# Feed-forward weight rounding placed from 3.0 instead of from 0 in a planned transformer layer

## The chip, the cores and the metric

The kernel runs on one core of a Trainium2 chip. The time is the device time of one launch in microseconds (us), as the median of several runs; lower is better. The core has a matrix engine (TensorE, PE in the profile, with its weight loads as PEld), a vector engine (DVE), a scalar engine (ACT), a general engine (GpSimd, POOL) and SyncE (SP), which here issues nearly all transfers. Every engine takes its instructions in the order in which they were traced. TensorE's clock is throttled at times, and the profile gives the granted share as PEclk.

## The reference, cut to what matters

One pre-norm layer on x of shape (2, 2048, 256): causal attention with 16 heads of 16, and a gated feed-forward of width 704, whose weights and inputs are rounded to blockwise FP4 values.

```python
x = x + attn(layernorm(x), Wq, bq, Wk, bk, Wv, bv, Wo, bo)   # rope on q and k, causal softmax
x = x + ffn(layernorm(x), w_gate, w_up, w_down)

def fp4_quant_dequant(x):            # blocks of 16 along the last dimension
    scale = max(max(abs(block)) / 6, 1e-12)
    q = nearest of (0, .5, 1, 1.5, 2, 3, 4, 6) to abs(block / scale), with its sign
    return q * scale
def fp4_linear(x, w):
    return fp4_quant_dequant(x) @ fp4_quant_dequant(w).T
h = silu(fp4_linear(x, w_gate)) * fp4_linear(x, w_up)
return fp4_linear(h, w_down)
```

## The kernel before, in words

**Tiling.** The sequence of each of the two batches b is cut into four chunks c of 512 rows (CH), each chunk into four tiles of 128. The 16 heads are in four groups g of four heads. A (batch, chunk, group) is one slot of the attention; there are 32 slots. A slot has two passes over the keys. The maximum pass (`max_steps`) multiplies queries and keys (`sc`, L1068, masked by L1037) and reduces each product to a row maximum on DVE (`mx` in chunk 0, `parts` in the others, L1092); the maxima are split in two parts (`mslots`, L1130 and L1133), turned (`ptm`, L1149) and copied (`mT`, L1153). The value pass (`value_steps`) computes the scores again less the maxima (`sx`, L1200 and L1208), takes the exponential on ACT (`ex`, L1223) and multiplies by the values (`av`, L1256).

**What a slot needs first.** Chunk by chunk, and in two blocks of eight heads each (blk), queries and keys are projected (`project_steps`): the matmul `pj` (L812), the bias on ACT (`qb`, L825), the cosine part on DVE (`t`, L832), a shuffle on DVE (L858), the sine part, a sum and a remainder on POOL (L864, L867, L894), then a trip through DRAM on the SP queue (`parts`, L904, and from there `qT`, L915, and `kT`, L928). The values are copied on DVE (`v`, L1003). The input rows are normalised in `norm_steps`, on DVE and POOL (`rstd`, L524).

**Rounding of the weights.** The three feed-forward weights are cut into 18 pieces (`weight_items`): six of `w_gate`, six of `w_up` and six of `w_down`, mostly 128 x 256. `load_rounded` gives each piece four steps: load (SP, `wr`, L649), scaled (DVE: L558, L561, L562; POOL: L566, L569), rounded (DVE: L585, L588; POOL: L591, L594, L597) and turn (two transposes on PE, `ptr`, L660, and copies on ACT, L680 or L690). A piece holds one of two buffers of kind `xn` from its load to its turn; the feed-forward of the rows uses the same two buffers later. The first matmul that reads a rounded weight is `pg` (L1548), in the feed-forward of the first chunk.

**The planner.** Nothing is issued at once. Each step calls `add` with an engine, an estimated cost, what it reads and writes, and a due place on one common list. `Plan.ordered` then goes through all tasks: it lets each engine take a task that can begin first, by its own estimates of costs, transfer landings (`landing`, 2.0 us and 1 us for each 250 KB) and free buffers; among those that can begin within PATIENCE = 0.03 us of the first, the lowest due goes first. A task is a candidate only if its due is at most AHEAD = 3 above the lowest due not yet done. The order found is the order of tracing, so on the chip each engine keeps it, whether the estimates held or not.

**Places.** Places are numbers, not microseconds. Slot n's maximum pass covers the places from `place[n]` to `place[n+1]`, its value pass begins 0.3 of a slot after that. The costs in the code give place 0 to 0.4 for slot 0, 0.4 to 1.4, 1.4 to 2.4 and 2.4 to 3.4 for slots 1 to 3 (the first chunk), 3.4 to 4.8 for slot 4, 4.8 to 6.8 for slot 5 and 6.8 to 8.8 for slot 6. Projections are placed between the slots that need them, for instance the first chunk's second block at 0.12 to 0.9 and the second chunk's first block at 1.7 to 2.9. The opening work has places from -10 to about -7. The 18 pieces are spread over 0 to WEIGHTS = 8: piece i covers a width of 1.9 shares from i shares, and one share is 8/19 = 0.42. The first chunk's feed-forward starts at place 8.2.

The change is in `layer_kernel`, in the lines that place the pieces:

```python
items = weight_items()
share = WEIGHTS / (len(items) + 1)
for i, steps in enumerate(items):
    side += placed(steps, i * share, (i + 1.9) * share)
```

Of the kernel before, what the change touches and what calls it, by code (L numbers as in the profile page):

```python
# [83 lines left out]
LATE = 4  # L84

WEIGHTS = 8

NUDGE = 1.0 - 1.5 * 2.0**-23

# [217 lines left out]
def layer_kernel(  # L307
# [364 lines left out]
    def weight_items():  # L672

        items = []
        for w, wT, target in ((w_gate, wgT, wg_), (w_up, wuT, wu_)):
            for row in range(0, I, P):
                rows = min(P, I - row)

                def put(pt, wT=wT, row=row, rows=rows):
                    nc.scalar.copy(wT[:, :, row : row + rows], pt[:, :, :rows])  # L680

                items.append(load_rounded(w, row, rows, 0, E, put, target))
        for row in range(0, E, P):
            for col in range(0, I, E):
                cols = min(E, I - col)

                def put(pt, row=row, col=col, cols=cols):
                    for k in range(0, cols, P):
                        n = min(P, cols - k)
                        nc.scalar.copy(  # L690
                            wdT[:n, (col + k) // P, row : row + P], pt[:n, k // P, :]
                        )

                items.append(load_rounded(w_down, row, P, col, cols, put, wd_))
        return items
# [991 lines left out]
    def placed(steps, lo, hi):  # L1687

        lags = [lag for lag, _ in steps]
        lags[0] = 0  # L1690
        at, out = 0, []
        for lag, step in zip(lags, (step for _, step in steps)):
            at += lag
            out.append((lo + (hi - lo) * at / max(sum(lags), 1), step))
        return out
# [17 lines left out]
    for n in range(slots):  # L1713
        steps, split, turn = max_steps(*order[n // NG], n % NG)
# [4 lines left out]
        steps, divide = value_steps(*order[n // NG], n % NG)  # L1719
# [6 lines left out]
    side = []  # L1726
# [10 lines left out]
        side += placed(project_steps(*order[k], blk), lo, hi)  # L1737
        done = hi
    items = weight_items()
    share = WEIGHTS / (len(items) + 1)  # L1740
    for i, steps in enumerate(items):
        side += placed(steps, i * share, (i + 1.9) * share)
    raw_o = []
    side.append((0.2, lambda due: raw_o.extend(load_plain(wo, "y", att, due))))
    side.append(
# [8 lines left out]
    ready = [divided[NG * k + NG - 1] + 0.01 for k in range(len(order))]  # L1754
    ready[0] = max(ready[0], WEIGHTS + 0.2)
    end = place[slots + 1]
    at = 0
    for k in range(len(order) - 1):
# [8 lines left out]
        share = (at - lo) / TPC  # L1767
# [37 lines left out]
    steps = [step for _, step in project_steps(*order[0], 0)]  # L1805
# [11 lines left out]
    def transpose_biases(due):  # L1817
# [46 lines left out]
        lambda due, i=i, pair=pair: steps[0].stripped(i, pair, due)  # L1864
# [73 lines left out]
```

## Time and profile before

| what | value |
|---|---|
| median of three runs (lowest to highest) | 1386.13 us (1380.96 to 1386.45) |
| time of the profiled execution | 1382.78 us |
| its span in the profile | 1381.0 us |
| PE busy | 1311.1 us, 95% of the span |
| DVE busy | 1115.0 us, 81% |
| ACT busy | 749.6 us, 54% |
| POOL busy | 538.2 us, 39% |
| mean granted clock of TensorE | 0.969 |
| first scaling of a weight piece on DVE (L558) | 24.8 us |
| last transpose of a weight piece (L660) | 174.5 us |
| first `pg` matmul (L1548) | 195.8 us |

The profiled execution's time is its span and 1.78 us around it. Busy time is a mean over stages with different limits, so the stage in which the weights are rounded, the first 175 us, has to be read by itself. The windows view gives, for each stretch, the busy time of each engine with the number of instructions, then the granted clock, the share in which the transfer engines were busy, and what they moved.

### The profile page before, as it was taken

Reading aid. Unit: us, or ns where it says so; the run is one execution under the profiler, and the core shown is the slowest. Engines: PE = TensorE matmul, PEld = TensorE weight load, DVE = VectorE, ACT = ScalarE, POOL = GpSimd, SP = SyncE. Lnnn points to the kernel's source line nnn. Section 1 sums busy time; section 2 is a strip of 40 time slices with the busy share of each in tenths; the row PEclk is TensorE's granted clock in tenths of the full one; section 3 lists DMA queues with packets and bytes.
Section 4 is the critical chain, followed back from the end, with each engine's and each line's share of the span. In section 5 each row is a group of like instructions: output and inputs, shape, how many; then the busy total and the mean of one; then the engine's idle time right before and its main releaser. Section 6 shows DMA issues by size and latency. Waiting matters only on the chain.

```text
span 1381.0 us, 27458 instructions
## 1 busy us (share of the span) xinstructions
PE 1311.1 (95%) x10269; PEld 653.7 (47%) x10269; DVE 1115.0 (81%) x2415; ACT 749.6 (54%) x1670; POOL 538.2 (39%) x685
## 2 busy tenths in 40 slices
PE   7887999999999999999998999999999999999977
PEld 4443454444544444444454555444454444444455
DVE  7787989988889998875478888996878978884286
ACT  3532655456655566557743555454655556667711
POOL 4654635434323434314344644432342332321360
PEclk8977999999999999999999999999999999999998
DMA  2544433321121401221444414240130130000000
GB/s 88 133 124 109 100 89 63 100 40 55 56 47 39 109 17 39 66 51 44 93 112 96 108 38 99 70 93 24 47 85 18 42 81 13 5 14 9 9 1 19
DMA packets 61886, 84.37 MB, mean 61 GB/s; under 512 B 14772, under 2 KB 30520, under 8 KB 61752
## 3 DMA queue, kind: packets, MB, share of 16 engines
q1 hardware_dynamic: 61744, 82.61, 24.4%
q8 instruction: 81, 1.33, 0.4%
q14 instruction: 53, 0.43, 0.1%
q10 hardware_dynamic: 8, 0.00, 0.0%
HBM read 55.09 MB, written 27.49 MB: 60 GB/s over the span
## 4 chain that ended last, share of the span: by engine, by line
PE 65%; DVE 20%; issue 5%; POOL 5%; DMA 2%; ACT 2%; SPq 0%; POOLq 0%; DVEq 0%; ACTq 0%
PE av L1256 15%; PE sc L1068 9%; PE pg L1548 9%; PE sx L1200 8%; DVE parts L1092 8%; PE sx L1208 7%; PE pd L1642 6%; PE pj L812 3%; PE pth L1407 2%; PE po L1492 2%; PE pv L994 1%; DVE scale L558 1%; DVE step L585 1%; PE sc L1037 1%; DVE step L588 1%
## 5 line engine op out<-in xcount | busy, mean ns | idle before, releaser
L1223 ACT ACTIVATE ex<-sx 128x512 f32<-128x512 f32 (+3 forms) x1280 | 592.6, 539 | 346.8 <-PE sx L1208 203.0
L1092 DVE TENSOR_REDUCE parts<-sc 128x1 f32<-128x512 f32 (+3 forms) x1152 | 638.5, 613 | 65.2 <-PE sc L1068 46.3
L1208 PE MATMUL sx<-qT,kT 64*128 64x512 f32 (+3 forms) x1280 | 338.0, 524 | 0.0
L1256 PE MATMUL av<-ex,v 128*32 128x512 f32 (+3 forms) x2560 | 301.1, 543 | 0.0
L1068 PE MATMUL sc<-kT,qT 64*128 64x512 f32 (+3 forms) x1280 | 288.6, 431 | 12.9 <-DMA kT<-parts 3.4
L1200 PE MATMUL sx<-mT,less 64*128 64x512 bf16 (+3 forms) x1280 | 250.7, 357 | 5.9 <-DVE parts L1092 2.2
L1068 PEld LDWEIGHTS sc<-kT,qT 64*128 64x128 f32 x1280 | 137.7, 191 | 173.0 <-DVE parts L1092 57.0
L1200 PEld LDWEIGHTS <-less 64*128 64x128 bf16 x1280 | 67.8, 94 | 212.4 <-issue 203.2
L566 POOL TENSOR_SCALAR inv<-inv 128x16 f32<-128x16 f32 (+2 forms) x82 | 17.6, 215 | 369.4 <-DVE inv L562 341.2
L1208 PEld LDWEIGHTS sx<-qT,kT 64*128 64x128 f32 x1280 | 133.2, 197 | 10.3 <-issue 7.7
L1642 PE MATMUL pd<-wdT,hrT 128*128 128x256 f32 (+1 forms) x384 | 104.8, 414 | 1.3 <-ACT hrT L1411 0.8
L1256 PEld LDWEIGHTS av<-ex,v 128*32 128x32 f32 x2560 | 52.7, 108 | 70.9 <-issue 60.5
L1642 PEld LDWEIGHTS pd<-wdT,hrT 128*128 128x128 f32 (+1 forms) x384 | 70.5, 198 | 29.5 <-issue 15.8
L864 POOL TENSOR_TENSOR t<-t,cs 128x512 f32<-128x512 f32 x31 | 39.8, 1285 | 112.3 <-DVE t L858 106.3
L1548 PE MATMUL pg<-wgT,xT 128*128 128x352 f32 x224 | 76.9, 476 | 0.9 <-ACT xT L1411 0.8
L812 PE MATMUL pj<-xnT,wqkT 128*128 128x512 f32 x128 | 74.1, 674 | 3.6 <-DVE v L1003 1.7
L1092 DVE TENSOR_REDUCE mx<-sc 128x1 f32<-128x128 f32 (+3 forms) x128 | 54.5, 479 | 26.4 <-PE sc L1037 26.2
L1548 PE MATMUL pg<-wuT,xT 128*128 128x352 f32 x224 | 74.4, 472 | 0.1
L1037 PE MATMUL sc<-pick,mask_q 64*128 64x64 bf16 x1024 | 70.5, 201 | 0.0
L591 POOL TENSOR_TENSOR h<-h,step 128x704 f32<-128x704 f32 x28 | 47.2, 1687 | 48.8 <-DVE step L588 41.0
L1037 PE MATMUL sx<-pick,mask_k 64*128 64x64 bf16 x1024 | 64.4, 198 | 0.0
L1574 ACT ACTIVATE h<-pg 128x352 f32<-128x352 f32 x64 | 29.8, 466 | 62.9 <-PE pg L1548 54.8
(156 smaller groups left out, 1534.2 us busy)
## 6 DMA issues: line engine op xcount, KB each, us to landing
qT<-parts SPq DMA_DIRECT2D x120, 128.0 KB
kT<-parts SPq DMA_DIRECT2D x120, 128.0 KB
parts<-high SPq DMA_DIRECT2D x30, 256.0 KB
parts<-t SPq DMA_DIRECT2D x30, 256.0 KB
sums<-avs SPq DMA_DIRECT2D x28, 256.0 KB
cs<-in_rope_dram SPq DMA_DIRECT2D x8, 512.0 KB
xin<-in_L_attn_x_dram SPq DMA_DIRECT2D x28, 128.0 KB
y<-sums SPq DMA_DIRECT2D x28, 128.0 KB
```

The costliest lines, as they stand in the source:

```text
L591: queue.tensor_tensor(src(), src(), st["step"], ALU.add)
L812: nc.tensor.matmul(got["pj"], lhsT=wqkT[:, k, i, cols], rhs=xnTs[b, c][:, k, :], start=(k == 0), stop=(k == KE - 1),)
L864: (nc.gpsimd if early and i == 0 else queue).tensor_tensor(swapped, swapped, angles[b, c][:, 1, :], ALU.mult)
L1037: nc.tensor.matmul(sc[h][:, col + at : col + at + STRIP], lhsT=strips(mask, h, half), rhs=strips(pick, h), start=False, stop=(half == 1),)
L1068: nc.tensor.matmul(sc[h][:, :cols], lhsT=strips(qT, h, d, slice(i * P, (i + 1) * P)), rhs=strips(kT, h, duo, slice(0, cols)), start=True, ...
L1092: nc.vector.tensor_reduce(dst, got[0][h][:, :cols], AX.X, ALU.max)
L1200: nc.tensor.matmul(sc[h][:, off:], lhsT=strips(less[d], h), rhs=strips(mT, h, slice(off, CH)), start=True, stop=False,)
L1208: nc.tensor.matmul(sc[h][:, off:], lhsT=strips(kT, h, duo, slice(jj, jj + P)), rhs=strips(qT, h, d, slice(off, CH)), start=False, stop=(j ...
L1223: nc.scalar.activation(st[j, d][:, h, off:], got[0][h][:, off:], AF.Exp, scale=HD**-0.5)
L1256: nc.tensor.matmul(st["av"][SLOT * s : SLOT * (s + 1), off:], lhsT=v[:, at : at + SLOT], rhs=st[j, d][:, h, off:], start=(j == 0), stop=(j ...
L1548: nc.tensor.matmul(got[half], lhsT=split("xrT")[:, k, :], rhs=wT[:, k, half * IH : (half + 1) * IH], start=(k == 0), stop=(k == KE - 1),)
L1642: nc.tensor.matmul(st["pd"], lhsT=st["hrT"][:n, k, :], rhs=wdT[:n, k, :], start=(k == 0), stop=(k == KI - 1),)
```

## The change

A constant FIRST = 3.0 is added. The 18 pieces are now spread over 3 to 8 instead of 0 to 8: one share is 5/19 = 0.263 instead of 0.421, and a piece's own four steps cover 0.5 instead of 0.8. Piece 0 goes from the places 0 to 0.8 to the places 3.0 to 3.5, piece 8 from 3.37 to 4.17 to 5.11 to 5.61, and piece 17 from 7.16 to 7.96 to 7.47 to 7.97. Steps, instructions, tiles and buffers are the same; only the dues that the planner sees differ.

```diff
 WEIGHTS = 8
+
+FIRST = 3.0
...
     items = weight_items()
-    share = WEIGHTS / (len(items) + 1)
+    share = (WEIGHTS - FIRST) / (len(items) + 1)
     for i, steps in enumerate(items):
-        side += placed(steps, i * share, (i + 1.9) * share)
+        side += placed(steps, FIRST + i * share, FIRST + (i + 1.9) * share)
```

## The prediction

> **What bounds the kernel now.** I read the page first. Over the span TensorE is the bound: PE is busy for 1311.1 of 1381.0 us, and what is left is little.
>
> ```profile
> span 1381.0 us, 27458 instructions
> ...
> PE   7887999999999999999998999999999999999977
> ...
> DVE  7787989988889998875478888996878978884286
> ...
> POOL 4654635434323434314344644432342332321360
> PEclk8977999999999999999999999999999999999998
> ```
>
> One digit is 34.5 us. PE falls short in the first four digits and the last two, and the clock in the first four. The change works in the first five, so I cut that stretch with the windows view at the events that matter: the first maximum reductions (24 us), the first key products of slot 2 (72), of slot 4 (107), the end of slot 4's maximum pass (about 138), the last weight transpose (175).
>
> ```profile
> 24.00:72.00 48.00, 40.36 (x350) 22.08 (x347) 33.43 (x90) 22.72 (x56) 28.85 (x42) 0.84 0.45 107
> 72.00:107.00 35.00, 32.09 (x316) 17.99 (x316) 29.40 (x77) 16.40 (x43) 20.14 (x29) 0.76 0.52 121
> 107.00:118.70 11.70, 8.18 (x39) 4.11 (x40) 6.15 (x18) 1.41 (x4) 5.54 (x9) 0.71 0.64 152
> 118.70:138.00 19.30, 13.84 (x73) 7.52 (x70) 18.96 (x44) 3.20 (x8) 5.83 (x11) 0.65 0.28 78
> 138.00:175.00 37.00, 34.72 (x304) 16.20 (x303) 34.67 (x90) 24.57 (x62) 25.16 (x42) 1.00 0.45 97
> ```
>
> The columns after the length are PE, PEld, DVE, ACT, POOL, then clock, transfer share and GB/s. From 24 to 107 no engine is full: PE idles 10.6 us, DVE 20.2 us. From 118.7 to 138 DVE is full (18.96 of 19.30) and PE idles 5.5 us at a clock of 0.65: here only the maximum pass of slot 4 can run. From 138 to 175 PE and DVE are both full (2.3 us idle each).
>
> **What a piece costs.** In the groups view up to 200 us the 18 pieces cost DVE 7.0 (L558) + 7.0 (L585) + 18/19 of 7.4 + 4.3 + 4.7 (L588, L561, L562, one of whose 19 belongs to the rows) = 29.5 us, or 1.64 us each; POOL 12.9 + 12.9 + 11.2 + 11.0 + 18/19 of 4.1 = 51.9 us, or 2.88 us each; PE two transposes (ptr, 8.2 us in all), 0.46 us each. By the times of ptr, nine pieces are finished before 107 us and nine after.
>
> **The change.** It removes no instruction. It moves the places of all 18 pieces later, the first by 3.0, piece 8 by 1.74, the last by 0.05. I calibrate places with the trace: slot 2 begins (place 1.4) at 72 us, slot 4 (3.4) at 107 us, slot 4's value pass (5.4) near 136 us, the last piece (7.96) at 175 us. So the 18 pieces' own places now lie at 107 to 175 us. They may begin earlier, since a task may start up to 3 places ahead of the lowest undone due, but only where an engine has nothing of lower due. At place 0.9 pieces 0 and 1 are admitted to their turn, at 2.4 pieces up to 7. Two buffers limit the rate too. DVE's free time from 72 to 107 would be 35.00 - 29.40 plus the weights' part of it, about 8 us, some 4 pieces less the gaps that are waits. I take 5 pieces done before 107 us instead of 9; the ends are 9 (all gaps used) and 2. So **4 pieces move**: 6.6 us of DVE and 11.5 us of POOL go behind 107 us.
>
> **What is gained before 107 us.** The clearest stall of the weights is this, in the timeline of DVE:
>
> ```profile
> 68.44 0.69 DVE L1003 TENSOR_TENSOR v<-pv,bvb 128x512 f32<-128x512 f32 x1 [2.47 <-PE pv L994]
> 72.41 0.41 DVE L558 TENSOR_REDUCE scale<-wr 64x16 f32<-64x256 f32 x1 [3.28 <-DMA wr<-in_L_ffn_w_gate_dram]
> ...
> 74.00 0.63 DVE L1003 TENSOR_TENSOR v<-pv,bvb 128x512 f32<-128x512 f32 x1
> ```
>
> Two scalings stand ahead of a `v` copy and wait for a load issued at 68.16, which lands 4.2 us later where the planner reckons 2.5. PE's next projection waits 1.74 us for that copy. The other waits of PE on weights up to 107 are 0.93 (ptr for POOL at 53.2), 0.27, 0.20 and 0.45 us. Sum 3.6 us; with 4 of 9 pieces gone from here I count the 1.74 and half the rest: **-2.7 us**. A further wait of 1.70 us, at 70.4 for `kT`, could shrink too: two roundings and a rescale of a piece (0.73 + 0.73 + 0.62) lie between that key block's POOL steps at 48.6 to 54.6. But SP then issues den, y and only then kT at 60.19, in order, behind a landing of sums. I count nothing there; at most 1.7.
>
> Then the clock. The Trainium skill (TensorE: Matmul & The Clock Gate, The HAM clock gate) says that some 3.4 us of sustained work release it. The row is harsher: from 80 to 90 us PE is busy 9.30 of 10 us and the granted clock is 0.50; one product of the projection takes 2.07 us for two instructions there against 1.02 at 97.8. By the rule a stall costs itself and a cold restart of 1.7 us; by the row the stalls at 70 to 75 cost some 7 us more, half of the 14 us from 75 to 90. I take neither into the sum, since kT's wait alone keeps PE still there; the row's 7 us belongs to the range.
>
> **What is lost after 107 us.** (a) Slot 4's maximum pass has places 3.4 to 4.8. At the old spacing 1.4 places hold 3.3 pieces, at the new 5.3: two more, with dues below those of much of the pass. The gaps at 107 to 118 (5.5 us of DVE) are waits for `kT`, a `wr` load and PE, so they take in part of this only. 2 x 1.64 = 3.3 us; DVE is the bound, PE waits: **+3.3**. The ends are 0 and 5. (b) From 138 to 175 two more pieces, 3.3 us, come on a DVE that has 2.3 us left, in pieces of at most 0.94 us that are waits for others. PE there alternates maximum and value passes and runs out of the second when the first is late: **+3.3**, ends 0 and 6. POOL has 25.16 of 37.00 and would get 5.8 more; the rope steps of later key blocks wait behind it.
>
> (c) The shared port. SBUF — State Buffer (Who interferes with whom) says that a DVE operation with two SBUF inputs, or in a two-port mode, and a POOL operation lock each other out for the whole instruction, while reductions never contend. The row agrees for one case: at 37.13 `left<-mx,mslots` takes 1.24 us against 0.19 median, beside the POOL sum of 37.07 to 38.33. By the rule each of 16 added POOL operations of up to 0.73 us could hold DVE, 11 us; by rows, the excess over the medians at L561, L585, L588, L1130 and L1133 from 107 to 175 is about 3.2 us for nine pieces. I take the rows, 4 x 0.36: **+1.4**. (d) SP. A `wr` load waits in SP's queue for one of the two buffers, and all transfers behind it wait too, `qT` and `kT` among them:
>
> ```profile
> SPq L649 <- PE ptr L660: 47.1, 7, 25.1
> ```
>
> That is 47.1 us in seven waits, 25.1 the longest, mostly while nothing else was ready. A piece comes every 3.8 us by its new places (0.263 of some 14.6 us a place, from 68 us over 4.6 places), and two buffers allowed one every 5 us (nine from 129.6 to 174.4), so loads will stand waiting more often. Priced as one wait like PE's for kT (1.7 us): **+1.7**, from 0 to 5. Its own arithmetic says that the pieces end late, by up to 13 x 5 = 65 us after 107, that is about 172, so `pg` at 195.8 still has about 20 us of cover; without it each us of delay would go to the end.
>
> Sum: -2.7 + 3.3 + 3.3 + 1.4 + 1.7 = **+7.0 us**. The profiled execution's 1382.8 becomes 1389.8. The median shown is 1386.1, 3.4 us above that execution, so the forecast stands at **1393 us**. After 210 us the order of issue will differ everywhere by small amounts with no direction that I can name; I give that 4 us either way.
>
> **Rivals.** *Release wins (faster).* With the pieces second in line, the chain of projections and slots 0 to 3 runs ahead: -3.6 for all PE waits on weights, -1.7 for kT, -7 for the clock of 75 to 90, while the pieces fill DVE's 20.2 us of idle time before 107 so that only two move, +3.3. Sum -9, so 1377. For it: the idle time exists and the planner lets lower places pass. Against it: much of that idle is DVE standing in order behind a load, and a filler brings the same stall elsewhere. *Nothing moves (no change).* The look-ahead of 3 equals the shift of 3.0, so every piece is admitted when the attention reaches its old place, engines are never left idle for a due, and gains and losses cancel: 1386. Against it: in conflicts the rank decides, and piece 0's rank changes by 3 whole places. *Starved first feed-forward (slower still).* If a piece takes over 6.5 us after 107 with 13 left, the last transpose passes 192 us and pg waits; from there +1 us for each us, say 1405.
>
> **Chances.** The main case (crowding) 0.46, at 1386 to 1405; release 0.28; no change 0.20; starving 0.06. What a measurement of this kernel can tell from no change is about 0.5%, 6.9 us. Nearly all of the starving and 0.38 of the crowding case are past it, so slower 0.44; of release 0.26 is past it; the rest, 0.30, is within. The range is 1371 (release, less 4 us of later order and 2 more of clock before 70 us) to 1407 (losses (a), (b) and (d) at their ends give 1401, and 4 of later order and 2 of starving).
>
> **What would show it.** Right: ptr transposes done before 107 us fall from 18 to about 10; DVE's wr share after 118 us rises; slot 4's first `sx` with 512 columns comes no earlier than 134.5 us; POOL above 30 of 37 us in the last stretch. Release is right if that first `sx` comes before 128 us and the clock stays near 1.0 from 70 to 90. I am wrong altogether if PE's idle time before 210 us is unchanged and the difference arises after it, or at the end of the span.

## The result, and the profile after

The changed kernel takes **1396.64 us** (median of 4 runs, 1396.34 to 1401.39) against 1385.2 us of before (4 runs beside them): ratio 1.0088, 95% interval 1.0065 to 1.0110. It is slower, by 11.4 us, and the interval lies wholly above 1. Its profiled execution took 1396.83 us, with a span of 1395.0 us against 1381.0. The mean granted clock is 0.969 in both. The two lines of FIRST move all later line numbers by 2.

The page, the rows that were shown of before (40 slices of 34.9 us, busy tenths):

```profile
span 1395.0 us, 27452 instructions
...
PE   7887899999999999999998999999999999999977
...
DVE  7677999988889988786368888997888989885286
...
POOL 3533764434224432234325555243442333321360
PEclk8887999999999999999999999999999999999999
```

The row of PE differs from before in one digit, the fifth slice (140 to 174 us), though the span is 14 us longer: the loss is spread too thin for this view. The windows view has the same columns as before (PE, PEld, DVE, ACT, POOL, clock, transfer share, GB/s):

```profile
24.00:72.00 48.00, 41.88 (x347) 24.31 (x345) 32.19 (x81) 22.05 (x54) 22.92 (x32) 0.75 0.43 92
72.00:107.00 35.00, 28.88 (x300) 17.30 (x302) 24.66 (x64) 14.65 (x37) 13.58 (x18) 0.80 0.51 124
107.00:118.70 11.70, 7.10 (x49) 3.54 (x41) 5.93 (x18) 2.15 (x7) 6.44 (x11) 0.76 0.70 157
118.70:138.00 19.30, 14.84 (x66) 7.63 (x65) 17.61 (x40) 2.24 (x5) 4.25 (x7) 0.68 0.27 75
138.00:175.00 37.00, 33.38 (x280) 15.56 (x279) 34.26 (x88) 22.93 (x54) 27.05 (x45) 0.92 0.46 95
```

From 72 to 107 us, where DVE and POOL were to be relieved, they are (DVE 24.66 for 29.40, POOL 13.58 for 20.14), but PE is not busier: 28.88 us for 32.09. From 118.7 to 175 us, where DVE was to be overfilled, it is no fuller than before (17.61 for 18.96, 34.26 for 34.67). The longest stall there is in the timeline of DVE:

```profile
71.19 0.69 DVE L1005 TENSOR_TENSOR v<-pv,bvb 128x512 f32<-128x512 f32 x1 [4.18 <-PE pv L996]
76.57 0.42 DVE L560 TENSOR_REDUCE scale<-wr 128x16 f32<-128x256 f32 x1 [4.68 <-DMA wr<-in_L_ffn_w_gate_dram]
...
78.33 0.42 DVE L560 TENSOR_REDUCE scale<-wr 128x16 f32<-128x256 f32 x1 [0.84 <-DMA wr<-in_L_ffn_w_gate_dram]
...
79.16 0.66 DVE L834 SCALAR_TENSOR_TENSOR t<-pj,bqk,cs 128x512 f32<-128x512 f32 x1
```

and in that of PE:

```profile
79.87 0.77 PE L1070 MATMUL sc<-kT,qT 64*128 64x256 f32 x2 [5.74 <-DVE t L834]
```

Two pieces end together (their `ptr` run at 70.99 us), so both buffers come free at once. The next two loads are issued at 72.09 and 74.11 us and land after 4.5 and 4.2 us; the planner reckons 2.5. Both scalings stand on DVE ahead of a rope step `t`, DVE idles 4.68 + 0.84 us, and PE stands 5.74 us behind `t`. Before had two waits in the same place, 1.74 us by a stall of the same make and 1.70 us for `kT`, so the net cost of the stall is some 2.3 us.

To see where the rest arises, I use one measure for all kernels, the **lag**: each matmul of TensorE is weighted with the median distance from its kind (tiles and shape) to the next start, over all traces, and the lag at T is how much later a kernel has done as much work as before had done at T. It compares the profiled executions, which are 14.0 us apart where the medians are 11.4. At 1340 us it agrees with the difference of the spans to 1.8 us in every kernel; at a single T it can jump by some 4 us, where a block of work is done in another order. After less before: +2.4 us at 80 us, +1.9 at 100, +6.0 at 110, +9.7 at 240, +16.7 at 620, +13.5 at 1340. An event that needs no weights agrees: the `mT` copy of slot 15 comes at 651.4 us for 634.6.

So there are three losses, about **6, 4 and 7 us**, and some 3 are given back. The first is only in part that stall. After it the changed kernel has nearly caught up: the product that waits for slot 4's `kT` starts at 109.56 us for 109.01. Then a transposition of a piece stands on PE ahead of the rest of slot 4's maximum pass and waits for the last POOL step of its rounding:

```profile
114.14 0.47 PE L662 MATMUL ptr<-ident,wr 64*128 64x64 f32 x2 [3.68 <-POOL wr L599]
```

In the same place before waited 0.28, 0.46 and 1.06 us. Slot 4's `mT` copy then comes at 135.1 us for 132.2. The rest of the 6 us is work put off: nine pieces were finished before 107 us, now five (10 `ptr` matmuls for 18). The last `ptr` is at 195.7 us for 174.5, and the first `pg` at 204.2 for 195.8.

### The profile page after: what moved, and what is told of

Its sections match the earlier page's. It is cut to its first block, busy times and chain, and to the rows that moved or that the text cites. A ratio compares the mean times of both kernels' runs of the same rounds, so it can differ in the third digit from the quotient of the medians.

```text
span 1395.0 us, 27452 instructions
## 1 busy us (share of the span) xinstructions
PE 1316.6 (94%) x10269; PEld 657.9 (47%) x10269; DVE 1121.1 (80%) x2415; ACT 750.4 (54%) x1670; POOL 538.1 (39%) x685
## 4 chain that ended last, share of the span: by engine, by line
PE 64%; DVE 22%; DMA 5%; issue 4%; POOL 3%; ACT 2%; SPq 1%; POOLq 0%; ACTq 0%; DVEq 0%
PE av L1258 15%; PE sc L1070 9%; PE pg L1550 9%; DVE parts L1094 9%; PE sx L1202 8%; PE sx L1210 7%; PE pd L1644 6%; PE pj L814 3%; PE pth L1409 2%; PE po L1494 2%; DVE step L587 1%; DVE mx L1094 1%; DMA kT<-parts 1%; ACT ex L1225 1%; DVE step L590 1%
## 5 line engine op out<-in xcount | busy, mean ns | idle before, releaser
L1202 PE MATMUL sx<-mT,less 64*128 64x512 bf16 (+3 forms) x1280 | 252.2, 358 | 10.4 <-DVE parts L1094 5.8
L1070 PEld LDWEIGHTS sc<-kT,qT 64*128 64x128 f32 x1280 | 140.6, 191 | 160.3 <-DVE parts L1094 53.1
L1210 PEld LDWEIGHTS sx<-qT,kT 64*128 64x128 f32 x1280 | 133.4, 197 | 12.0 <-issue 10.5
L525 POOL TENSOR_SCALAR ve<-mv 128x1 f32<-128x1 f32 x64 | 12.7, 199 | 148.3 <-DVE mv L521 145.4
```

What stands on the lines that cost most here:

```text
L1070: nc.tensor.matmul(sc[h][:, :cols], lhsT=strips(qT, h, d, slice(i * P, (i + 1) * P)), rhs=strips(kT, h, duo, slice(0, cols)), start=True, ...
L1202: nc.tensor.matmul(sc[h][:, off:], lhsT=strips(less[d], h), rhs=strips(mT, h, slice(off, CH)), start=True, stop=False,)
L1210: nc.tensor.matmul(sc[h][:, off:], lhsT=strips(kT, h, duo, slice(jj, jj + P)), rhs=strips(qT, h, d, slice(off, CH)), start=False, stop=(j ...
```

## The experiments

All ratios are to before, in runs beside it. My first theory was the prediction's: after 107 us the pieces crowd DVE, POOL and SP. The first rival was that the planner's landing estimate makes the stall at 74 to 80 us and with it the loss, the second that the loss is made by the order of issue alone.

**Which half of the pieces?** Pieces 0 to 8 moved and the others left, and the reverse:

```diff
-        side += placed(steps, i * share, (i + 1.9) * share)
+        near = (WEIGHTS - 3.0) / (len(items) + 1)
+        if i < 9:                                  # early_half; late_half: i >= 9
+            side += placed(steps, 3.0 + i * near, 3.0 + (i + 1.9) * near)
+        else:
+            side += placed(steps, i * share, (i + 1.9) * share)
```

> The kernel before with pieces 0 to 8 at the places of the change (3.0 to 5.6) and pieces 9 to 17 at their old places. Crowding theory (cost of pieces after 138 us): the lag behind before at the release of slot 7 is under 6 us and the time 1386 to 1391. Late-load theory (the 5.7 us stall of PE at 74 to 80 us costs the first 5 us): the stall is there again, the lag is some 5 us by 110 us. Order theory: any time from 1383 to 1400, with the difference arising after 240 us.

> The kernel before with pieces 0 to 8 at their old places and pieces 9 to 17 at the places of the change (5.4 to 8.0, later and denser). Crowding theory: no lag by 130 us, then a lag of 4 to 8 us by the release of slot 7, time 1389 to 1394. Late-load theory: lag under 3 us at slot 7, time 1384 to 1389. Order theory: any time from 1383 to 1400, with the difference arising after 240 us.

Measured: early_half 1395.94 us, ratio 1.0075 [1.0049, 1.0102]; late_half 1386.54, 1.0018 [1.0007, 1.0030]. The two shares add up to 0.93%, the whole change cost 0.88%, and by the totals most of it goes with the first nine pieces. The windows view of 110 to 175 and 175 to 240 us, first before, then late_half, then early_half:

```profile
110.00:175.00 65.00, 55.55 (x398) 27.06 (x399) 59.52 (x150) 28.52 (x69) 33.61 (x58) 0.84 0.41 99
175.00:240.00 65.00, 63.92 (x544) 32.17 (x542) 57.41 (x126) 37.16 (x84) 27.08 (x30) 1.00 0.31 75
```

```profile
110.00:175.00 65.00, 59.25 (x437) 30.73 (x436) 61.28 (x157) 30.95 (x73) 34.43 (x58) 0.84 0.39 96
175.00:240.00 65.00, 63.34 (x538) 30.67 (x536) 57.45 (x123) 36.64 (x84) 26.58 (x31) 1.00 0.37 89
```

```profile
110.00:175.00 65.00, 54.35 (x362) 26.38 (x362) 60.22 (x144) 25.28 (x57) 36.00 (x59) 0.79 0.40 93
175.00:240.00 65.00, 62.80 (x538) 31.15 (x536) 57.50 (x136) 37.16 (x89) 31.50 (x45) 1.00 0.33 79
```

With the dense second half of the change, late_half does more matmuls from 110 to 175 us than before (437 for 398), and its lag at 240 us is -4.5. The denser late places do no harm by themselves; late_half loses 7.1 us from 240 to 620. early_half has the stall again (5.21 us, ending at 78.37), but its lag is +2.0 at 110 us. It loses 5.8 us between 110 and 180, ahead of its first `pg` (205.0) and of that of before (195.8), so a late `pg` isn't the cause there, and from 180 us on its lag stays within 1 us. Stage by stage the halves don't add up: the whole change is at +9.7 by 240 us, where the halves are at +7.8 and -4.5, and of the two only late_half has its loss after 240 us. The near agreement of the totals is no proof of one cause. (The profiled execution of early_half took 1390.04 us, its quickest; the lag of its trace shows less than its median.)

**Is it the time of the rounding instructions?** The plan is kept, and the DVE and POOL instructions of the 18 pieces' rounding are not issued, in both kernels, so the rounding of the weights is left out:

```diff
+            kept = (lambda run: lambda: None) if bare else (lambda run: run)
-            add(DVE, on_vector(n) + 0.36 + 0.005 * nb, sizes, [thing], [small16], due)
+            add(DVE, on_vector(n) + 0.36 + 0.005 * nb, kept(sizes), [thing], [small16], due)
...
-        scaled, rounded = fp4(lambda: st["raw"], raw, rows, cols)
+        scaled, rounded = fp4(lambda: st["raw"], raw, rows, cols, bare=True)
```

> The kernel before with its plan and order unchanged, but none of the DVE and POOL instructions that round the 18 weight pieces are issued (the weights stay unrounded; loads, transposes and copies stay). Crowding theory: before had room for part of the rounding, so this gains 8 to 14 us on before. Order theory (the two kernels differ mainly because the planner lays out the later slots differently): the gain is the same as that of the matching kernel after.

> The changed kernel with its plan and order unchanged, again without the DVE and POOL instructions that round the pieces (weights unrounded). Crowding, or a late load ahead of DVE: the 11 us between the two kernels shrink to under 4 us, since no DVE instruction of a piece is left to be late or in the way; the lag at the release of slot 7 (mT), 13.3 us now, falls under 4. Order theory: 8 to 14 us of difference stay, and the lag that arises after 260 us (some 5 us) stays.

Measured: bare_before 1376.47 us, 0.9951 [0.9928, 0.9975]; bare_after 1388.27, 1.0024 [1.0012, 1.0036]. All 18 roundings cost 7.9 us in the old places and 8.4 in the new (0.49% and 0.64% by the ratios). If crowding made the difference of 11.4 us, it would have gone with them; without them the two kernels are 11.8 us apart by the medians, 0.73% by the ratios for 0.88. The crowding theory falls as the main cause. The order theory had expected the same saving in both, and 8 to 14 us of difference. What the instructions do explain is most of the first loss: where nothing stands waiting for a step of a piece, the lags at 110 us are -1.9 (bare_before) and -0.6 (bare_after). Between 110 and 240 us the changed order still loses 3.7 us against the old one, and between 240 and 620 us 6.0, much as the whole kernels do. Two stretches of equal work (that of 110 to 240 us of before, in before and then in after) show how the loss looks there:

```profile
110.00:240.00 130.00, 119.47 (x940) 59.23 (x940) 116.93 (x275) 65.68 (x151) 60.69 (x88) 0.92 0.36 87
116.00:249.70 133.70, 123.28 (x937) 60.14 (x936) 122.07 (x287) 66.69 (x154) 70.69 (x105) 0.92 0.38 86
```

DVE has 5.1 us and POOL 10.0 us more to do, but PE has no more gaps than before (10.4 us for 10.5). The loss is in matmuls that follow each other more slowly (123.3 us busy for 119.5), and this view doesn't say what holds them. The windows of 70 to 90 us, after and then bare_after:

```profile
70.00:80.00 10.00, 4.26 (x35) 2.70 (x31) 3.14 (x10) 2.44 (x5) 2.86 (x6) 0.95 0.50 134
80.00:90.00 10.00, 9.62 (x76) 7.55 (x76) 9.90 (x32) 0.77 (x2) 1.72 (x3) 0.50 0.36 114
```

```profile
70.00:80.00 10.00, 7.14 (x62) 5.98 (x63) 6.61 (x17) 0.69 (x1) 0.00 (x0) 0.55 0.42 122
80.00:90.00 10.00, 9.76 (x93) 5.99 (x97) 6.44 (x21) 5.51 (x13) 3.82 (x3) 0.60 0.45 120
```

**Is there a dose?** FIRST at 0.05, 1 and 2:

```diff
-FIRST = 3.0
+FIRST = 0.05      # first_005; first_1: 1.0; first_2: 2.0
```

> FIRST = 0.05 in place of 3.0: pieces are moved by at most 0.05 of a place against before, less than one piece. Crowding or late load: 1384 to 1386, no lag behind before anywhere. Order theory (the planner's layout answers small shifts with differences of several us): any time between 1378 and 1394, with PE's order differing from before within the first 200 us.

> FIRST = 1.0. If a later start costs by what it does to the engines, the time rises in step with FIRST: some 4 us over before, 1387 to 1390. Order theory: no step, any time between 1378 and 1397.

> FIRST = 2.0. Cost in step with FIRST: some 8 us over before, 1391 to 1394. Order theory: no step, any time between 1378 and 1397.

Measured: 1387.89 us, 1.0021 [1.0007, 1.0036]; 1401.31, 1.0117 [1.0088, 1.0146]; 1406.14, 1.0154 [1.0120, 1.0187]. A shift of a sixtieth of the change's already costs 0.2% and 3.4 us of lag by 110 us, and the shifts of 1 and 2 cost more than that of 3. The loss does not grow with the distance: each shift makes another order. In first_1 and first_2 the lag is 6.6 and 7.8 us by 80 us already, without that stall: the longest waits of their PE from 24 to 80 us, 3.75 and 3.76 us, are for `mslots` of slot 1, up to 55.6 and 57.1 us.

**Is it the landing estimate?** The planner reckons 5.0 us for a piece's load, in the changed kernel (land5_after), in before, and in early_half; and a version with the first half in place and the second half moved half as far (land5_mid):

```diff
-            add(SP, landing(128), run, [], [raw], due)
+            add(SP, 5.0, run, [], [raw], due)
```

> The changed kernel with the planner told that a piece's load lands 5.0 us after its issue instead of 2.5 (4.2 to 4.5 measured). Late-load theory: the 5.7 us stall of PE at 74 to 80 us shrinks under 2 us, the lag by 110 us from 6 us to 2 or less, the whole time to 1388 to 1394. Crowding or order theory: no gain by 110 us beyond 2 us, whole time anywhere from 1385 to 1402.

> The kernel before with only the landing of a piece's load set to 5.0 us; PE's order from slot 8 on is layout B. Late load plus layout theory: PE's 1.7 us wait for the v copy at 73 us is gone, 0 to 5 us ahead of before by 240 us, then 4 to 9 us lost by 620 us: 1385 to 1392. If the layout does not matter: 1379 to 1384.

> Pieces 0 to 8 at the places of the change, pieces 9 to 17 at their old ones, and the planner told 5.0 us for the landing of a piece's load. In PE's order the projections and value passes of slots 8 to 13 stand as in before (layout A; the changed kernel and all with a later last half have another one, B, and lost 4 to 10 us between 240 and 620 us). Late load plus layout theory: no stall at 70 to 80 us, no loss after 240 us, 1379 to 1386. If layout A is not what spares the loss after 240 us: 4 us or more are lost there and the time is 1388 to 1397. Crowding theory (later pieces cost DVE): 1388 to 1394, lost between 110 and 240 us.

> Pieces 0 to 8 at their old places, pieces 9 to 17 half way to the places of the change, landing 5.0 us; PE's order is layout A again. Late load plus layout theory: ahead of before by 3 to 6 us at 240 us, nothing lost after, 1377 to 1384, the fastest so far. If layout A is not what spares the loss: 4 us or more lost from 240 to 620 us, 1385 to 1392.

Measured: land5_after 1394.93 us, 1.0079 [1.0048, 1.0110]; land5_before 1391.77, 1.0052 [1.0035, 1.0069]; land5_early 1398.41, 1.0086 [1.0063, 1.0110]; land5_mid 1382.91, 0.9991 [0.9981, 1.0001]. In land5_after the stall is gone, as the rival has it:

```profile
70.00:80.00 10.00, 8.37 (x75) 6.31 (x75) 6.60 (x16) 2.43 (x5) 4.74 (x6) 0.81 0.47 129
80.00:90.00 10.00, 9.62 (x81) 6.58 (x82) 9.09 (x29) 4.11 (x9) 4.20 (x5) 0.51 0.47 119
```

PE is busy 8.37 us from 70 to 80 where the changed kernel has 4.26, and the lag at 110 us is +2.0 for +6.0. But the median falls by 1.7 us only, which the intervals don't tell from nothing: the new order loses 6.3 us between 110 and 240 us. land5_early was expected at 1379 to 1386 and missed by 12 us, with 15 us lost in that stretch, and before itself becomes slower with the better estimate, within the time that its theory had expected, though its lag at 240 us is +4.8, where it was to be ahead. So the stall is real, and its removal is no cure: the last `ptr` slips to 207.7 us in land5_after and to 214.8 in land5_early. land5_mid, the best of all and expected 3 to 6 us ahead at 240 us, cannot be told from before.

**Late or dense?** All pieces from 3, as far apart as before the change:

```diff
-WEIGHTS = 8
+WEIGHTS = 11      # with FIRST = 3.0
```

> The changed kernel with the second end of the list of times at 11 instead of 8: the 18 pieces start at slot 3 and stand as far apart as before the change (0.47 of a slot where the change has 0.29), and the rounding ends at slot 11 (which the last pieces' readers, the feed-forward of the first slots, have to wait for). This parts lateness of the first pieces from density. If the loss between 110 and 240 us comes from density, the work done by TensorE is no further behind before at 240 us than at 110 us, and the total is 1383 to 1390. If it comes from the first nine pieces being late, the loss of 4 us or more between 110 and 240 us stays. If only the laid-out order decides, neither holds with certainty and the order after 240 us (which of two sequences of projections it shows) sets the end, 1385 to 1402. The stall of 5 to 6 us before 110 us is expected wherever two pieces' loads are issued together just ahead of the softmax of slot 1; with wider places it may go. The rival that the place of the last feed-forward weight matters expects 1395 or more with an idle TensorE after 200 us.

(The two distances in it should read 0.42 and 0.26, 8/19 and 5/19.) Measured: 1393.22 us, 1.0071 [1.0041, 1.0101]. No such stall: the lag is -1.8 us at 110 us and -3.4 at 180, so the late and widely spaced first half loses nothing there. Then it loses 12 us from 180 to 240, in the windows of later_all:

```profile
200.00:210.00 10.00, 9.46 (x100) 3.98 (x98) 4.67 (x9) 6.47 (x17) 3.36 (x4) 1.00 0.91 129
210.00:220.00 10.00, 8.74 (x72) 4.39 (x66) 9.20 (x24) 3.73 (x11) 3.96 (x8) 0.83 0.06 22
220.00:230.00 10.00, 9.02 (x40) 4.85 (x40) 9.42 (x23) 3.26 (x6) 1.73 (x3) 0.61 0.09 20
```

The last `ptr` is at 217.3 us and the first `pg` at 236.1. The value pass of slot 6 has its last scores at 212 us with no feed-forward to take its place, and PE is left with the maximum pass of slot 7, which goes at DVE's pace (9.42 of 10 us): 40 matmuls from 220 to 230 us for 100 from 200 to 210. That looks like the starved first feed-forward of the prediction's third rival, but `pg` does not read the last pieces, which are of `w_down`. It reads `w_gate` and the first rows. These take a buffer of the pieces at 205.69 us, just after a piece's `ptr` at 204.97 (before at 176.26 after 174.49), and then their own rounding stands on DVE behind twenty reductions:

```profile
216.96 10.45 DVE L1094 TENSOR_REDUCE parts<-sc 128x1 f32<-128x512 f32 x20
...
227.49 0.23 DVE L587 TENSOR_SCALAR step<-xn 128x256 int32<-128x256 int32 x1
```

So of the 40 us by which `pg` is later than in before, some 29 go with the buffer and 10 with the order on DVE. No run parts the two.

**All whole kernels in one table.** Lag in us against before; "clock" is the mean granted clock over the work that before does from 110 to 240 us (0.92 there); "order" is the number of projections `pj` between the `mT` copies of slots 7 to 13, A = 0 8 0 7 1 7 1 as before, B = 4 4 0 8 0 5 3 as in the changed kernel, C = 4 4 4 4 0 7 1.

| kernel | `ptr` before 107 us | lag 110 | 240 | 620 | 1340 | clock | first `pg`, us | order | ratio |
|---|---|---|---|---|---|---|---|---|---|
| after | 10 | +6.0 | +9.7 | +16.7 | +13.5 | 0.92 | 204.2 | B | 1.0088 |
| early_half | 10 | +2.0 | +7.8 | +7.8 | +7.3 | 0.90 | 205.0 | A | 1.0075 |
| land5_after | 10 | +2.0 | +8.3 | +13.0 | +13.2 | 0.88 | 211.5 | B | 1.0079 |
| land5_early | 10 | +3.0 | +18.0 | +19.9 | +19.5 | 0.86 | 219.3 | A | 1.0086 |
| later_all | 10 | -1.8 | +8.7 | +13.6 | +12.2 | 0.84 | 236.1 | C | 1.0071 |
| first_1 | 13 | +5.8 | +11.8 | +18.5 | +18.3 | 0.87 | 208.5 | B | 1.0117 |
| first_2 | 12 | +12.9 | +16.9 | +24.8 | +25.1 | 0.89 | 211.0 | B | 1.0154 |
| late_half | 18 | -1.0 | -4.5 | +2.6 | +2.6 | 0.92 | 192.2 | B | 1.0018 |
| first_005 | 18 | +3.4 | +4.6 | +4.2 | +4.1 | 0.88 | 200.4 | A | 1.0021 |
| land5_mid | 16 | +0.6 | +0.0 | -0.1 | -1.4 | 0.90 | 197.3 | A | 0.9991 |
| land5_before | 16 | +0.9 | +4.8 | +11.4 | +7.6 | 0.88 | 195.3 | B | 1.0052 |

Two things part the rows. The seven kernels that have six and a half pieces or fewer done before 107 us lie at 1.0071 to 1.0154, the four with eight or nine at 0.9991 to 1.0052. Each of the seven is 3.7 to 15 us further behind at 240 us than at 110 us, but land5_before, with eight pieces done, is too (3.9 us), and the seven also have the latest first `pg`. So the table doesn't say which of these is the cause. And from 240 to 620 us every kernel of order B loses a further 4.7 to 7.9 us, where those of order A change by -0.4 to +1.9 and the one of order C loses 4.9.

The clock is a rival for 110 to 240 us that no run tests. In the changed kernel it explains nothing, 0.92 for 0.92; between bare_before and bare_after (0.92 and 0.90) it could be up to 3 of the 3.7 us. In land5_early and later_all it could be much of the loss: a clock of 0.86 over 145.0 us and of 0.84 over 140.5 us takes away some 20 and 22 us of full clock for 10 in before. Whether the low clock is cause or effect of the thinner work there is not shown.

What makes order B slow is seen only in part. PE's waits from 240 to 620 us, before and then after:

```profile
PE sc L1068 <- ACT ex L1223: 1.2, 2, 0.7
...
PE sx L1200 <- DVE parts L1092: 0.3, 1, 0.3
```

```profile
PE sx L1202 <- DVE parts L1094: 2.1, 7, 0.4
PE sc L1070 <- ACT ex L1225: 1.6, 3, 0.6
PE sc L1070 <- DVE parts L1094: 1.3, 4, 0.7
```

The value pass stands in line behind the maximum pass more often (2.1 us in seven waits for 0.3 in one). The whole list sums to 7.4 us for 5.1, so such waits make 2.3 us of the 7.0. A stretch of 3.4 us at half clock, which every kernel of order B in the table has between 458 and 483 us and none of order A has from 300 to 620, can take up to 1.7 us more. In after it is this:

```profile
471.50:474.90 3.40, 3.40 (x20) 1.65 (x19) 3.40 (x8) 1.31 (x3) 2.06 (x2) 0.50 0.81 254
```

The rest is in score products that follow each other more slowly, and stays open.

The 3 us given back after 620 us are not the order's. Between 1100 and 1150 us the trace of before has a stretch at half clock:

```profile
1107.50:1114.30 6.80, 6.80 (x38) 3.94 (x36) 5.02 (x13) 1.55 (x6) 4.11 (x5) 0.50 0.27 80
```

late_half, first_005 and land5_mid, of both orders, have none there and each gain some 2.8 us on before; early_half and land5_after have one as long and gain nothing; after has 3.4 us and gains 1.3. So this part of the lag is the clock of single executions.

## Why the prediction was right, point by point

The direction and the size were right: slower, 1396.64 us where 1393 was forecast. The mechanism was mostly not. What the sum priced at +8.0, crowding, did not come about, and what it left without a direction, the later order, brought +7.0. That the number came so near is luck.

- **Five pieces before 107 us, four move: right**, 10 `ptr` matmuls. (The last piece moves by 0.32 of a place at its start and 0.02 at its end, not by 0.05; nothing in the sum rests on it.) Moving the first nine pieces alone costs 0.75%.
- **Gain of 2.7 us before 107 us: not there.** The stall on `v` went, but one of 5.74 us came at 74 to 80 us, for 1.70 + 1.74 before. The lag is +1.9 at 100 us, and +6.0 at 110 with the wait of 3.68 us for POOL behind it. The argument that the prediction put against its release rival, that a filler brings the same stall elsewhere, held for the main case also. bare_after, with the order unchanged, shows that it is the pieces' steps that PE stood behind; land5_after fits the landing estimate as the reason why the plan put them there.
- **Clock, left out of the sum: right.** Up to the same work at 110 us the granted clock is 0.84 before and 0.83 after. The row was also right against the rule of 3.4 us: half clock lasted 13.6 us with PE busy (the last section has the line).
- **Crowding, (a), (b) and (c), 8.0 us together: wrong.** Not issuing the rounding saves 7.9 us in the one kernel and 8.4 in the other, so the new places make it dearer by 0.5 us (2 by the ratios, within their intervals) and not by 8, and late_half runs the denser last pieces without harm. The lag does grow by 3.7 us between 110 and 240 us, but in bare_after as well (3.7 against bare_before), where no rounding takes any time. The sign that DVE's share for the pieces rises after 118 us came true (twelve roundings for eight) without the cost that it was to show. POOL, forecast above 30 of 37 us from 138 to 175, has 27.05.
- **(d), SP's queue, +1.7: not settled.** The waits in the queue for a piece's buffer are more and shorter:

```profile
SPq L651 <- PE ptr L662: 42.3, 11, 11.4
```

  42.3 us in eleven for 47.1 in seven from 24 to 210 us, the longest 11.4 for 25.1. No run took this queue away by itself.
- **The later order, "4 us either way": under-sized.** It is +7.0 us from 240 to 620 us, by a sequence of projections that lies wholly behind the moved pieces. Which order a plan falls into could not be told from the profile of before.
- **Cover of `pg`, some 20 us: too large**, 8.5 us are left (195.7 to 204.2), since the last piece ends at 195.7, not at 172. The rate was misread: from 129.6 to 174.4 before ends eight pieces, not nine, one in 6.4 us and not in 5. Thirteen pieces at that rate end at about 190. `pg` itself waits for nothing: 0.04 us, and 8.4 us late at a lag of 7.1 at 200 us. The third rival took `pg` to wait for the last transpose, and the kernel passed its mark of 192 us without starving.
- First `sx` with 512 columns of slot 4 no earlier than 134.5: right, it is at 136.3 us, but 135.1 in before, so this sign speaks only against release.
- **Release wins** is refuted for the change (lag +6.0 at 110). A gain of its kind exists: later_all has the same five pieces done, is 1.8 us ahead at 110 us and has slot 4's `mT` at 125.1 us for 132.2, and pays it back later.
- **Nothing moves** is refuted: 18 `ptr` became 10.
- **"Wrong altogether" if PE's idle time before 210 us is unchanged and the difference arises later: half so.** PE idles 5.2 us more up to the work of 110 us, but 8.8 of the 16.7 us of lag at 620 us arise after 210.

What is shown: the time of the rounding instructions is not the main cause; the pieces' steps make the two waits of PE before 115 us; the kernels of order B lose 4.7 to 7.9 us from 240 to 620 us. What stays open: which step out of line makes the 3.7 us between 110 and 240 us in the changed kernel, and most of what makes order B slow. A late first `pg` is ruled out for early_half, where the loss stands by 180 us; in the changed kernel the lag is +8.2 by then, so that little is left for it.

## What to carry to other kernels

In a program whose order is laid out by a planner, a shift of fillers is not priced by their busy time alone: ask which in-order instruction will now stand ahead of the critical one when its load or another engine's result comes late, compare the planner's landing estimate with the landings in the trace, and subtract what the kernel before paid in the same place (a stall of 5.74 us was worth some 2.3). The kernels that left the early gaps emptier were the slower ones here, 0.7 to 1.5%, but why is shown for none of them in full. Check a derived measure against an event that needs none, and the clock of both traces, before a late gain or loss is given a cause. And before a difference under one per cent is explained, shift the same knob by next to nothing: here 0.05 of a place moved the time by 0.2%, and a removed stall of 5.7 us came back as 1.7 us, which the intervals don't tell from nothing.

## What the runs showed of the hardware

The granted clock did not follow the busy time of PE from window to window. In the changed kernel PE stood for most of 74.1 to 79.9 us, and the clock stayed full up to 79; then it was half for 13.6 us, with PE busy nearly throughout. The second line is before, the third land5_after, which has no such stall:

```profile
79.00:92.60 13.60, 12.34 (x99) 9.27 (x99) 12.40 (x37) 3.37 (x7) 4.27 (x6) 0.50 0.29 91
73.20:90.30 17.10, 14.92 (x97) 8.95 (x98) 15.46 (x47) 3.46 (x8) 8.41 (x12) 0.50 0.43 126
76.20:89.90 13.70, 13.32 (x119) 10.32 (x121) 12.70 (x40) 4.77 (x11) 4.10 (x5) 0.50 0.48 126
```

So the stall of 5.74 us did not cost its length and a longer cold stretch on top. In later_all the clock was 0.61 over 220 to 230 us with PE busy 9.02 of 10, where few products but scores were left. And in nearly equal work late in the span, a stretch at half clock came in one execution and not in another (6.8 us at 1107.5 in before, none there in late_half), which moved the lag by 2.8 us.
